# Kept-weight sums from the sorted list, shorter tie and flag arithmetic, and gathered row maxima in a top-p attention step

## The chip, the cores and the metric

The kernel runs on one core of a Trainium2 chip. A core has five engines with one instruction queue each: TensorE (PE, with its weight loads shown apart as PEld), VectorE (DVE), ScalarE (ACT), GpSimd (POOL) and SyncE (SP), which here only issues transfers. The engines wait for each other with semaphores. The metric is the device time of one execution in microseconds; the number that counts is the median of several runs.

## What is computed

The reference is a stack of four graph layers on x (4096 x 256) with a 4096 x 4096 adjacency matrix; each is followed by a residual addition and a layer norm. The change lies in the second layer, which makes two attention steps:

```python
q = X @ W1.T @ W2.T;  k = X @ W3.T
probs = softmax(q @ k.T)                        # 4096 x 4096
sp = probs sorted in falling order per row
keep_sorted = cumsum(sp) - sp < 0.9             # top-p
A = probs * mask;  A = A / max(A.sum(-1), 1e-12)
Xf = R @ Xf;  Xa = A @ Xa;  Z += Xf @ U1[n].T + Xa @ U2[n].T
```

So each row keeps its largest weights until they hold 0.9 of the mass, of several equal weights at the border only the first ones, and is divided by the sum of what it kept. The other three layers are products with the adjacency matrix, a dense product and a layer norm.

## The kernel before

**Tiles.** The 4096 rows are worked in 32 tiles of 128 rows; a row of weights `e` has 4096 columns and 24 of padding. A step n (0 or 1) is one call of `run_step` (L944). Its loop over i works on three tiles at once: logits of tile i+2 on PE (L415, copied out of PSUM by ACT, L416), selection in tile i+1, products of tile i (`pieces`, L725: transposes on PE L746, copy by ACT L749, products L769), and between them products with the adjacency rows (`neighbours`, L688, ACT cast L685) for the other term.

**Selection in a tile of step 1.** `peak_groups` (L461) takes the 8 largest of each of 18 groups of a row (MAX8, L434), and from these the row's maximum m (L466), which L467 negates for the exponential. `exp_rows` (L446) has ACT make exp(e - m) with its sum z (L457). `tops` (L518) sorts the 72 largest candidates with nine rounds of MAX8 (L529) and MATCH_REPLACE8 (L533). `pick` (L535) runs a prefix sum over them (L551), finds the border weight t (L554 to L557), the number `left` of weights equal to t that must go (L559, L560), and a flag `bad` (L563, L564, L566) that is set where the list of 72 or the eight places for ties do not suffice. `flag` (L584) counts the flagged rows with two small matmuls (L594, L595), gives each a slot (L597, L601, L602) and POOL scatters their row numbers to a list in DRAM (L608). `settle` (L643) makes up to eight copies of t out of `left` (L656 to L658), strikes as many ties out of `e` (MATCH_REPLACE8, L660), zeroes all below t in four pieces with a sum each (L665), adds the sums (L668), and `whole` (L578) turns the total into the row's factor `sc` (L580, L582). In step 0 the tiles go another way: 16 candidates are sorted, 13 neighbours gathered, and the sum `kept` comes from the list already.

**Put-off rows.** Rows flagged bad are put off into jobs of 128 rows (`put_off`, L897): one job in step 0, three in step 1, of which two run inside the loop and the last after it. `take_rows` (L883) reads 128 list entries (`to_l`, L888), limits them to a valid row number (`from_l`, L890), and gathers the rows on POOL (L812). The job computes its logits anew, takes the maximum over all 4096 columns (`peak`, L470: L472, L473), the exponential, closes in on the border with five passes of `bracket` (L475, each pass L499), sorts and picks with 64 candidates, has up to 24 tie places (three L660), and here a flag of its own (PE L590) decides a branch to a slow path. `left_over` (L924) is for more rows than the jobs hold.

**Order.** A job is a generator; `run_step` advances it by one stage at given groups of `pieces` (about L1011 to L1033). After the loop `finish` runs the last job beside 32 tiles of `zu` products (L871) for the next layer, whose operands come by SP. Within this written order a scheduler of the framework arranges the instructions of each engine when the program is built, from its own estimates of durations; the resulting order is fixed on each engine.

Of the kernel before, what the change touches and what calls it, by code (L numbers as in the profile page):

```python
# [11 lines left out]
F32 = mybir.dt.float32  # L12
# [7 lines left out]
ALU = mybir.AluOpType  # L20
AX = mybir.AxisListType
# [3 lines left out]
P = 128  # L25
# [22 lines left out]
PAD = 8 * MATCHES_LATER  # L48
# [9 lines left out]
def gnn_stack(ctx, tc, x, adjt, adjn, w0, b0, w1, w2t, w3t, u1t, u2t, ln_g, ln_b, w2, b2, w3, b3, out):  # L58
# [3 lines left out]
    nc = tc.nc  # L62
    N = x.shape[0]
    NT = N // P
# [4 lines left out]
    J0 = min(4, NT)  # L69
    BITS_LO = int(np.array(0.09 / N, np.float32).view(np.int32))  # L70

    const = ctx.enter_context(tc.tile_pool(name="const", bufs=1))
    xpool = ctx.enter_context(tc.tile_pool(name="xpool", bufs=1))
    hpool = ctx.enter_context(tc.tile_pool(name="hpool", bufs=1))
    work = ctx.enter_context(tc.tile_pool(name="work", bufs=2))
    dram = ctx.enter_context(tc.tile_pool(name="dram", bufs=1, space=DRAM))
# [46 lines left out]
    adj8_d = [dram.tile([P, NT, P], F8, name=f"adj8_{it}_d") for it in range(NT)]  # L123
    h_d = dram.tile([N + P, D], F32, name="h_d")
    k_d = dram.tile([N + P, P], F32, name="k_d")


    blank = const.tile([P, NT], I32, name="blank")
# [3 lines left out]
    def rows(t, it):  # L132
        return t[it * P : (it + 1) * P, :]
# [89 lines left out]
    with tc.tile_pool(name="l0", bufs=1) as l0, tc.tile_pool(name="l0w", bufs=2) as l0w:  # L223
# [12 lines left out]
        for c in range(NT // J0):  # L236
            t = l0.tile([P, J0, D], F32, tag="in", name="x_in", bufs=SLOTS_IN)
# [11 lines left out]
            nc.scalar.dma_start(w3t_sb[:, :, h * DA : (h + 1) * DA], w3t.rearrange("(c p) o -> p c o", p=P))  # L249
        for t in list_d:  # L250
            nc.sync.dma_start(t[:N, :].rearrange("(p k) o -> p (k o)", k=NT), blank)
        x1 = xpool.tile([P, NT, D], F32, tag="X", name="x1")
        y0h = hpool.tile([P, NT, 2 * D], F32R, tag="H", name="y0h")
        deg1 = l0.tile([P, NT], F32, name="deg1")
# [103 lines left out]
    with tc.tile_pool(name="l1", bufs=1, reuse_waits="tile") as l1:  # L358

        cur = {"late": False, "n": 0, "nef_done": False}  # L360
# [10 lines left out]
        upto = l1.tile([P, PAD], F32, name="upto")  # L371
# [45 lines left out]

        def logits_in(l):

            nc.vector.memset(l[:, N:], -1.0)  # L420
            return l

        def small(tag, w=1, dt=F32, bufs=2):
            if cur["late"]:
                return cur["lw"].tile([P, w], dt, tag=tag, name=f"{tag}_l", bufs=2 if w == 1 else 1)
            return work.tile([P, w], dt, tag=tag, name=tag, bufs=bufs)
# [15 lines left out]
        def sparse(st):  # L442

            return cur["n"] == 0 and st["tile"] is not None
# [16 lines left out]
        def peak_groups(st, ngr=ngr):  # L461

            st["cand"] = cand = small("cand", 8 * ngr, bufs=1)
            groups(st["e"], cand, ngr, -(-N // ngr))
            st["m"] = m = small("m")
            nc.vector.tensor_reduce(m, cand, axis=AX.X, op=ALU.max)  # L466
            nc.vector.tensor_scalar(m, m, -1.0, None, op0=ALU.mult)  # L467
            st["base"] = None

        def peak(st):  # L470
            st["m"] = m = small("m")
            nc.vector.tensor_reduce(m, st["e"][:, :N], axis=AX.X, op=ALU.max)  # L472
            nc.vector.tensor_scalar(m, m, -1.0, None, op0=ALU.mult)  # L473

        def bracket(st):  # L475

# [58 lines left out]
        def pick(st, rounds):  # L535

            top, thr, base = st["top"], st["thr"], st["base"]  # L540
            W = 8 * rounds
            cs = small("cs", W + 1, bufs=1)
            if base is None:
                nc.vector.memset(cs[:, 0:1], 0.0)
                te = small("te", W + 1)
                nc.scalar.activation(te, top, AF.Exp, bias=st["m"], scale=1.0)
            else:
                nc.vector.tensor_copy(cs[:, 0:1], base)
                te = top
            nc.vector.memset(cs[:, W:], 3e38)  # L550
            nc.vector.tensor_tensor_scan(cs[:, 1:W], te[:, : W - 1], te[:, : W - 1], cs[:, 0:1], op0=ALU.add, op1=ALU.max)  # L551
            under, part = small("under", W, bufs=1), small("part", W, bufs=1)
            count = small("count")
            nc.vector.tensor_scalar(under, cs[:, :W], thr, 0.0, op0=ALU.is_lt, op1=ALU.add, accum_out=count)  # L554
            nc.vector.scalar_tensor_tensor(part, cs[:, 1:], thr, under, op0=ALU.is_ge, op1=ALU.mult)
            st["t"] = t = small("t_thr")
            nc.vector.scalar_tensor_tensor(part, part, 1.0, te[:, :W], op0=ALU.mult, op1=ALU.mult, accum_out=t)  # L557
            st["left"] = left = small("left")
            nc.vector.tensor_scalar(part, te[:, :W], t, 0.0, op0=ALU.is_ge, op1=ALU.add, accum_out=left)  # L559
            nc.vector.tensor_sub(left, left, count)  # L560
            st["bad"] = bad = small("bad")
            last = KEPT if sparse(st) else W - 1
            nc.vector.tensor_tensor(bad, te[:, last : last + 1], te[:, W:], op=ALU.max)  # L563
            nc.vector.tensor_tensor(bad, bad, t, op=ALU.is_ge)  # L564
            most = 0.0 if sparse(st) else 8.0 * (MATCHES if base is None else MATCHES_LATER)
            nc.vector.scalar_tensor_tensor(bad, left, most, bad, op0=ALU.is_gt, op1=ALU.max)  # L566
            if sparse(st):

                same = small("same")
                for r in range(8, W, 8):  # L570
                    nc.vector.tensor_tensor(same, top[:, r - 1 : r], top[:, r : r + 1], op=ALU.is_equal)
                    nc.vector.tensor_tensor(bad, bad, same, op=ALU.max)
                st["w"] = w = small("w", W)
                kept = small("kept")
                nc.vector.scalar_tensor_tensor(w, te[:, :W], t, te[:, :W], op0=ALU.is_ge, op1=ALU.mult, accum_out=kept)
                whole(st, kept)

        def whole(st, kept):  # L578

            nc.vector.tensor_scalar(kept, kept, 1e-12, None, op0=ALU.max)  # L580
            st["sc"] = sc = small("sc")
            nc.vector.reciprocal(sc, kept)  # L582
# [60 lines left out]
        def settle(st, loop=False):  # L643

            e, t, left = st["e"], st["t"], st["left"]
            if loop:
                bit_by_bit(st)
            elif st.get("later") is None:
                v = nc.vector.value_load(st["nb"][0:1, 0:1])
                with tc.If(v > 0):  # L650
                    bit_by_bit(st)

            M = 8 * (MATCHES if st["base"] is None else MATCHES_LATER)
            if not loop:
                go, no, match = (small(k, PAD, bufs=1)[:, :M] for k in ("go", "no", "match"))
                nc.vector.tensor_scalar(go, upto[:, :M], left, None, op0=ALU.is_lt)  # L656
                nc.vector.tensor_scalar(no, go, -1.0, None, op0=ALU.add)
                nc.vector.scalar_tensor_tensor(match, go, t, no, op0=ALU.mult, op1=ALU.add)  # L658
                for k in range(0, M, 8):
                    nc.vector.match_replace(st["e"], match[:, k : k + 8], st["e"], 0.0)  # L660
                    yield
            kq = small("kq", NQ)
            for c in range(NQ):
                q = slice(c * QW, (c + 1) * QW)
                nc.vector.scalar_tensor_tensor(e[:, q], e[:, q], t, e[:, q], op0=ALU.is_ge, op1=ALU.mult,  # L665
                                               accum_out=kq[:, c : c + 1])
            kept = small("kept")
            nc.vector.tensor_reduce(kept, kq, axis=AX.X, op=ALU.add)  # L668
            whole(st, kept)
# [213 lines left out]
        def take_rows(n, slots, e):  # L883


            st = {"tile": None, "e": logits_in(e)}
            st["to"] = to = small("to", 1, I32)
            nc.sync.dma_start(to, list_d[n][slots, :])  # L888
            st["from"] = fr = small("from", 1, I32)
            nc.vector.tensor_scalar(fr, to, float(N - 1), None, op0=ALU.min)  # L890
            return st, gathered(xa_d if n else x1_d, st, "xf_new")

        def all_logits(st, q):
# [3 lines left out]
        def put_off(n, k, e, later):  # L897


            base = work.tile([P, 1], F32, tag="base", name="base", bufs=2)  # L900
            nc.vector.tensor_scalar(base, later["base"], float((k + 1) * P), None, op0=ALU.max)
            later["base"] = base
            st, xg = take_rows(n, slice(k * P, (k + 1) * P), e)
            yield
            q = query(xg)
            if n:
                yield
            all_logits(st, q)
            yield st
            if n == 0:  # L910
                peak_groups(st)
                exp_rows(st)
            else:
                peak(st)
                exp_rows(st)
                yield
                yield from bracket(st)
            tops(st, 8)
            pick(st, 8)
            flag(st)  # L920
            yield
            yield from settle(st)
# [309 lines left out]
```

## Time and profile before

| | |
|---|---|
| median of three runs | 3057.41 us (3055.0 to 3058.85) |
| the profiled execution, its own time | 3159.93 us |
| its span, first to last instruction | 3158.2 us |
| mean granted TensorE clock | 0.971 |
| busy: PE, DVE, ACT, POOL | 2895.0, 2247.3, 1723.6, 678.1 us |
| step 0 of the attention, about | 375 to 1260 us |
| hand-over to step 1 | 1260 to 1375 us |
| loop of step 1 | 1375 to 2450 us |
| its tail, last job and zu products | 2450 to 2605 us |
| layers 2 and 3 | 2605 to 3158 us |

The profile is of one execution, which was longer than the median by a factor of 1.0335. Times in it are from the span's start. "idle <-X" says how long an engine stood still before an instruction and what ended it; a duration is not the price of an instruction where the next one starts before it ends, so prices here are taken from start to start where two neighbours are shown.

### The profile page before, as it was taken

What the parts mean: (1) busy time and instruction counts of PE and PEld (TensorE: products, weight loads), DVE (VectorE), ACT (ScalarE), POOL (GpSimd) and SP (SyncE); (2) the same over time, 40 slices, a digit from 0 to 9 for tenths busy, and PEclk for the clock granted to TensorE, in tenths of its full rate; (3) what the DMA queues carried; (4) which work ended last, traced back from release to release, by engine and by line L of the source; (5) the groups of instructions that cost most, each with busy time, mean ns of one, the idle gap of its engine ahead of it and who ended that gap; (6) DMA issues with size and microseconds to landing.
All of it is one profiled execution on the core that took longest, in us unless ns stands there. A gap on an engine that the chain in (4) does not pass through costs nothing. (4 is left out here: it accounts for less than half of the span.)

```text
span 3158.2 us, 44761 instructions
## 1 busy us (share of the span) xinstructions
PE 2895.0 (92%) x14052; PEld 2271.4 (72%) x14052; DVE 2247.3 (71%) x7159; ACT 1723.6 (55%) x2883; POOL 678.1 (21%) x812
## 2 busy tenths in 40 slices
PE   7999888999999997789998999999999987999998
PEld 3788656777777775567777777878877645777886
DVE  4666667888888876267998999967999644444444
ACT  3555545566666654465554655546555425666664
POOL 1121245555555554000000000010000110000000
PEclk9999989999999998899999999999999998999999
DMA  9996455777777774240000111011110324333332
GB/s 172 158 178 126 77 100 110 122 131 132 128 130 136 132 133 132 79 110 17 26 23 26 30 35 38 29 36 32 34 38 24 104 92 158 108 108 95 107 109 77
DMA packets 242873, 286.82 MB, mean 91 GB/s; under 512 B 32928, under 2 KB 199776, under 8 KB 242624
## 3 DMA queue, kind: packets, MB, share of 16 engines
q0 software_dynamic: 41728, 91.69, 22.1%
q1 hardware_dynamic: 188656, 180.93, 18.6%
q10 hardware_dynamic: 12240, 11.23, 1.1%
q8 instruction: 114, 1.87, 0.2%
q14 instruction: 135, 1.11, 0.2%
HBM read 318.06 MB, written 66.32 MB: 122 GB/s over the span
## 5 line engine op out<-in xcount | busy, mean ns | idle before, releaser
L688 PE MATMUL acc_r<-xh,adjq 128*128 128x512 f32 x2048 | 625.9, 434 | 33.2 <-ACT adjq L685 17.5
L769 PE MATMUL acc_bank<-xa,at 128*128 128x256 f32 x2240 | 551.0, 386 | 26.2 <-ACT at L749 25.8
L685 ACT CAST adjq<-adj 128x512 fp32r<-128x512 fp8e4 x512 | 315.5, 619 | 371.0 <-PE acc_r L688 214.6
L688 PEld LDWEIGHTS acc_r<-xh,adjq 128*128 128x128 f32 x2048 | 382.8, 193 | 132.0 <-ACT adjq L685 37.7
L674 POOL DMA_INDIRECT G<-x_d,cols x416 | 403.5, 970 | 326.0 <-PE acc_bank L763 172.2
L769 PEld LDWEIGHTS acc_bank<-xa,at 128*128 128x128 f32 x2240 | 409.9, 193 | 85.9 <-ACT at L749 37.5
L416 ACT COPY e<-lg 128x512 f32<-128x512 f32 x544 | 315.1, 586 | 231.2 <-PE lg L415 159.9
L434 DVE MAX8 cand<-e 128x8 f32<-128x228 f32 (+1 forms) x1088 | 385.0, 399 | 34.4 <-ACT e L416 31.7
L415 PE MATMUL lg<-kS,q 128*128 128x512 f32 x1088 | 391.6, 442 | 6.0 <-issue 3.8
L200 POOL TENSOR_TENSOR rstd<-ve,mhalf 128x1 f32<-128x1 f32 x166 | 100.3, 604 | 1331.8 <-DVE ve L198 1246.3
L1112 ACT CAST a<-a 128x1024 fp32r<-128x1024 fp8e4 x256 | 268.3, 1049 | 165.4 <-PE acc L176 127.1
L531 DVE FIND_INDEX8 cols<-top,e 128x8 uint32<-128x4096 f32 x64 | 282.8, 4419 | 0.0
L176 PE MATMUL acc<-xh,a 128*128 128x512 f32 x1024 | 260.1, 407 | 21.2 <-DMA a<-adj_d 16.1
L176 PE MATMUL acc<-y0h,a 128*128 128x512 f32 x1024 | 249.9, 397 | 0.0
L176 PEld LDWEIGHTS acc<-xh,a 128*128 128x128 f32 x1024 | 191.7, 190 | 67.8 <-ACT xh L152 23.5
L176 PE MATMUL acc<-yh,a 128*128 128x512 f32 x1024 | 237.9, 394 | 0.0
L763 PE MATMUL acc_bank<-G,dg 128*128 128x256 f32 x832 | 228.1, 392 | 8.3 <-DVE dg L761 4.1
L176 PEld LDWEIGHTS acc<-yh,a 128*128 128x128 f32 x1024 | 192.2, 188 | 43.8
L176 PEld LDWEIGHTS acc<-y0h,a 128*128 128x128 f32 x1024 | 187.9, 188 | 39.0 <-issue 0.6
L749 ACT COPY at<-at_ps 128x512 f32<-128x512 f32 x288 | 168.7, 588 | 84.7 <-PE at_ps L746 83.0
L415 PEld LDWEIGHTS lg<-kS,q 128*128 128x128 f32 x1088 | 183.4, 193 | 29.6 <-ACT e L416 9.2
L763 PEld LDWEIGHTS acc_bank<-G,dg 128*128 128x128 f32 x832 | 156.3, 195 | 38.6 <-DVE dg L761 4.5
(287 smaller groups left out, 4414.1 us busy)
## 6 DMA issues: line engine op xcount, KB each, us to landing
adj<-adj_d SPq DMA_DIRECT2D x256, 128.0 KB
a<-adj_d SPq DMA_DIRECT2D x256, 128.0 KB
a<-in_adjt POOLq DMA_DIRECT2D x64, 256.0 KB
adj_d<-a SPq DMA_DIRECT2D x64, 256.0 KB
adjn<-in_adjn POOLq DMA_DIRECT2D x64, 256.0 KB
x_d<-x SPq DMA_DIRECT2D x64, 128.0 KB
xf_d<-xf_new SPq DMA_DIRECT2D x64, 128.0 KB
xf<-xf_d SPq DMA_DIRECT2D x64, 128.0 KB
```

What stands on the lines that cost most here:

```text
L176: nc.tensor.matmul(acc, a[:, j, :], halves(jt), start=(jt == 0), stop=(jt == NT - 1))
L415: nc.tensor.matmul(pl[:, :LC], q[k], kS[:, s], start=(k == 0), stop=(k == 1))
L416: nc.scalar.copy(l[:, s], pl[:, :LC])
L434: nc.vector.max(dst[:, 8 * g : 8 * g + 8], src[:, g * w : min((g + 1) * w, N)])
L531: nc.vector.max_index(st["at"][:, 8 * r : 8 * r + 8], t8, st["e"][:, :N])
L674: nc.gpsimd.indirect_dma_start(out=g, out_offset=None, in_=x1_d, in_offset=bass.IndirectOffsetOnAxis(ap=st["at"][:, k : k + 1], axis=0))
L685: nc.scalar.copy(a, cur["a8"][:, g % 2 * GP : (g % 2 + 1) * GP, :])
L688: nc.tensor.matmul(acc_r, a[:, j, :], xf[:, jt, :], start=(jt == 0), stop=False)
L749: nc.scalar.copy(at[:, :G, :], ps[:, :G, :])
L763: nc.tensor.matmul(acc_a, dg[:, k % 4, :], st["G"][k], start=(k == 0), stop=(k == KEPT - 1))
L769: nc.tensor.matmul(acc_a, ats[g][:, j, :], cur["xa"][:, jt, :], start=(jt == 0), stop=(jt == NT - 1))
L1112: nc.scalar.copy(a, a8)
```

## The change

The change has five parts, all in the second layer:

- `peak_groups` and `peak` let the reduction write the negated maximum itself, without the multiplication by -1. In step 1 `peak_groups` also writes the 128 maxima to a new tensor `m_d` in DRAM, on SP's queue; the tensor is cleared once at the start.
- `put_off` of step 1 gathers the maxima of its 128 rows from `m_d` on POOL, and `peak` isn't called there any more (`left_over` still calls it).
- `pick` computes `bad` in one instruction instead of two, and for the tiles of step 1 the sum of the kept weights from the sorted list, with `under` as mask, and `sc` from it. The four L665 of these tiles have no sum, and L668 is gone for them; jobs keep both.
- `settle` makes the tie places in one instruction (`upto < left` times t): places not used hold 0 instead of -1, and the padding of `e` is set to 0 instead of -1.
- `take_rows` limits the row number with a bitwise and instead of a minimum.

```diff
+        nc.sync.dma_start(m_d.rearrange("(p k) o -> p (k o)", k=NT), blank.bitcast(F32))
...
-            nc.vector.memset(l[:, N:], -1.0)
+            nc.vector.memset(l[:, N:], 0.0)
...
-            nc.vector.tensor_reduce(m, cand, axis=AX.X, op=ALU.max)
-            nc.vector.tensor_scalar(m, m, -1.0, None, op0=ALU.mult)
+            nc.vector.tensor_reduce(m, cand, axis=AX.X, op=ALU.max, negate=True)
+            if cur["n"]:
+                nc.sync.dma_start(rows(m_d, st["tile"]), m)
...
-            nc.vector.tensor_tensor(bad, te[:, last : last + 1], te[:, W:], op=ALU.max)
-            nc.vector.tensor_tensor(bad, bad, t, op=ALU.is_ge)
+            nc.vector.scalar_tensor_tensor(bad, te[:, last : last + 1], te[:, W:], t, op0=ALU.max, op1=ALU.is_ge)
...
+            elif st["tile"] is not None:
+                kept = small("kept")
+                nc.vector.scalar_tensor_tensor(part, under, 1.0, te[:, :W], op0=ALU.mult, op1=ALU.mult, accum_out=kept)
+                whole(st, kept)
...
-                go, no, match = (small(k, PAD, bufs=1)[:, :M] for k in ("go", "no", "match"))
-                nc.vector.tensor_scalar(go, upto[:, :M], left, None, op0=ALU.is_lt)
-                nc.vector.tensor_scalar(no, go, -1.0, None, op0=ALU.add)
-                nc.vector.scalar_tensor_tensor(match, go, t, no, op0=ALU.mult, op1=ALU.add)
+                match = small("match", PAD, bufs=1)[:, :M]
+                nc.vector.scalar_tensor_tensor(match, upto[:, :M], left, t.to_broadcast([P, M]), op0=ALU.is_lt, op1=ALU.mult)
...
+            if st["tile"] is not None:
+                for c in range(NQ):
+                    q = slice(c * QW, (c + 1) * QW)
+                    nc.vector.scalar_tensor_tensor(e[:, q], e[:, q], t, e[:, q], op0=ALU.is_ge, op1=ALU.mult)
+                return
...
-            nc.vector.tensor_scalar(fr, to, float(N - 1), None, op0=ALU.min)
+            nc.vector.tensor_scalar(fr, to, N - 1, None, op0=ALU.bitwise_and)
...
+            if n:
+                st["m"] = m = small("m")
+                nc.gpsimd.indirect_dma_start(
+                    out=m, out_offset=None, in_=m_d, in_offset=bass.IndirectOffsetOnAxis(ap=st["from"][:, 0:1], axis=0))
...
             else:
-                peak(st)
                 exp_rows(st)
```

The negation in `peak` (L472, L473) is folded in the same way. In the new file the reduction of `peak_groups` stands at L470; the lines below it are shifted by a few. The prediction uses the old numbers, and L470 for that reduction where it speaks of the write to `m_d`.

More of the change, by code (lines that the diff above doesn't have):

```diff
@@ L70, in gnn_stack @@
     BITS_LO = int(np.array(0.09 / N, np.float32).view(np.int32))
+    assert N & (N - 1) == 0
     const = ctx.enter_context(tc.tile_pool(name="const", bufs=1))
@@ L125, in gnn_stack @@
     k_d = dram.tile([N + P, P], F32, name="k_d")
+    m_d = dram.tile([N, 1], F32, name="m_d")
     blank = const.tile([P, NT], I32, name="blank")
@@ L471, in peak @@
             st["m"] = m = small("m")
-            nc.vector.tensor_reduce(m, st["e"][:, :N], axis=AX.X, op=ALU.max)
-            nc.vector.tensor_scalar(m, m, -1.0, None, op0=ALU.mult)
+            nc.vector.tensor_reduce(m, st["e"][:, :N], axis=AX.X, op=ALU.max, negate=True)
         def bracket(st):
@@ L572, in pick @@
                     nc.vector.tensor_tensor(bad, bad, same, op=ALU.max)
+            elif st["tile"] is not None:
+                kept = small("kept")
+                nc.vector.scalar_tensor_tensor(part, under, 1.0, te[:, :W], op0=ALU.mult, op1=ALU.mult, accum_out=kept)
+                whole(st, kept)
+            if sparse(st):
                 st["w"] = w = small("w", W)
```

## The prediction

> **What bounds the kernel now.** I first read the page's busy times, because they say which engine can matter at all.
>
> ```profile
> PE 2895.0 (92%) x14052; PEld 2271.4 (72%) x14052; DVE 2247.3 (71%) x7159; ACT 1723.6 (55%) x2883; POOL 678.1 (21%) x812
> ```
>
> TensorE (PE) is busy 92% of the span, VectorE (DVE) 71%; by this average no DVE edit would count. The average hides the stages, so next come the stretches. Columns: length, then busy time of PE, PEld, DVE, ACT, POOL with counts, granted clock, DMA share.
>
> ```profile
> 375.00:1260.00 885.00, 790.88 (x4223) 606.99 (x4221) 698.86 (x2100) 516.77 (x1001) 476.63 (x512) 0.95 0.70 127
> 1448.00:1682.00 234.00, 216.25 (x1139) 181.56 (x1139) 213.53 (x746) 121.13 (x202) 18.05 (x24) 1.00 0.08 24
> 1988.00:2064.00 76.00, 74.36 (x389) 62.53 (x388) 73.53 (x264) 44.28 (x74) 5.91 (x7) 1.00 0.09 28
> 2440.00:2605.00 165.00, 147.00 (x601) 96.09 (x599) 94.00 (x208) 56.55 (x115) 22.04 (x20) 0.98 0.28 95
> 2605.00:3158.00 553.00, 517.98 (x2240) 413.43 (x2240) 245.42 (x656) 330.97 (x425) 36.18 (x65) 0.97 0.35 109
> ```
>
> The rows are: attention step 0; eight tiles of step 1 ahead of any put-off job; three tiles between two jobs; the tail of step 1; layers 2 and 3. In step 1 PE and DVE are both nearly full. In the second row both have about 20 us of holes in 234, so the two wait for each other in a ring; in the third row DVE has 2.5 us free in 76 and PE 1.6, so what DVE saves, PE can use only up to its own holes. In the tail DVE has much room, but one chain of it is what PE ends up waiting for. The last row is untouched.
>
> Then the groups by line, for step 1 with its hand-over: which DVE work is there to take.
>
> ```profile
> L665 DVE SCALAR_TENSOR_TENSOR e<-e,t_thr 128x1024 f32<-128x1024 f32 x128 | 159.0, 1276 | 0.0
> ...
> L472 DVE TENSOR_REDUCE m_l<-e 128x1 f32<-128x4096 f32 x3 | 13.3, 4420 | 23.9 <-ACT e L416 23.9
> ```
>
> The timeline of DVE in a tile without a job shows the chain that the change shortens; the durations overlap, so prices are read from start to start.
>
> ```profile
> 1505.71 0.23 DVE L656 TENSOR_SCALAR go<-upto,left 128x8 f32<-128x8 f32 x1
> 1505.97 0.17 DVE L657 TENSOR_SCALAR no<-go 128x8 f32<-128x8 f32 x1
> 1506.18 0.23 DVE L658 SCALAR_TENSOR_TENSOR match<-go,t_thr,no 128x8 f32<-128x8 f32 x1
> 1506.51 0.09 DVE L660 MATCH_VALUE_LOAD e<-match,e 128x8 f32 x1
> ```
>
> Last the tail's timeline, of DVE and of PE, around the last put-off job.
>
> ```profile
> 2458.45 0.15 DVE L890 TENSOR_SCALAR from_l<-to_l 128x1 int32<-128x1 int32 x1 [7.23 <-DMA to_l<-list_d]
> ...
> 2475.57 4.42 DVE L472 TENSOR_REDUCE m_l<-e 128x1 f32<-128x4096 f32 x1 [10.71 <-ACT e L416]
> 2480.02 0.15 DVE L473 TENSOR_SCALAR m_l<-m_l 128x1 f32<-128x1 f32 x1
> 2484.10 0.15 DVE L459 TENSOR_SCALAR thr_l<-z_l 128x1 f32<-128x1 f32 x1 [3.93 <-ACT e L457]
> ...
> 2535.12 0.16 DVE L566 SCALAR_TENSOR_TENSOR bad_l<-left_l,bad_l 128x1 f32<-128x1 f32 x1
> ```
>
> ```profile
> 2535.33 0.19 PE L590 MATMUL mm_bank<-ones_col,bad_l 128*1 128x1 f32 x2 [1.41 <-DVE bad_l L566]
> ...
> 2566.89 1.04 PE L746 MATMUL at_ps<-ident,e 128*128 128x128 f32 x8
> ```
>
> Logits are done at 2475.6, then 4.4 us row maximum, 3.9 us exponential (ACT), 51 us bisection and sorting, then the flag matmul L590. PE fills this time with other work in a written order, waits 1.41 us at L590, and does 31.4 us more before the job's products at 2566.9.
>
> **What the Trainium skill says.** "Vector Engine (DVE) Microarchitecture Reference", section 5.2, gives 1.0417 ns per column plus about 75 ns per instruction; 1024 columns would be 1.14 us. The trace has 1.20 from start to start, and 1.20 for L513 too, which has no accumulator; so dropping the accumulator of L665 gains nothing, although the page shows a separate read of 83 ns. "DMA: Bandwidth & Descriptors", "Anatomy of one DMA", puts about 2 us on every transfer, mostly the receipt; here a scatter, its receipt and the read back (L608 at 2447.30 to L890 at 2458.45) take 11.2 us. "TensorE: Matmul & The Clock Gate", "What's actually happening", halves the clock after an idle window of about 3.4 us; the trace agrees: after a PE gap of 4.00 us at 2088.5 eight L769 matmuls took 3.78 us instead of 1.89.
>
> **The change part by part**, from start-to-start times and from the order of instructions of the two programs, which is fixed when they are built.
>
> *Tiles without a job* (about 8). The chain L564 (1505.33) to L660's load (1506.51) loses L657 (0.21), L656 and L658 become one (about 0.3), L563/L564 become one; the new sum (72 wide, like L557: 0.23, with a read) stands in gaps of the chain and takes back about 0.15. Ahead of it L467 goes (0.12). Ring shorter by 0.5: 8 x 0.55 = -4.4.
>
> *Dense tiles* (about 16). Saved pitches: L467 0.12, L563/564 0.06, L656/657/658 0.23, L668 0.08; added 0.18 for the sum. -0.3 x 16 = -4.8, all usable only if PE's holes (about 1 us a tile) give way. Those of L594, which waits for "bad", give least: the new sum stands just ahead of L566.
>
> *Step 0.* L467 and L564 of 32 tiles, 0.13 a tile, PE waits about 1 us a tile on flags: -2, at most -4.
>
> *Row maxima* (3 times 4.42). In the two jobs inside the loop DVE's next instructions in the new order are thr_l and the first probe, ahead of the tile's last maxima; they wait for the exponential, 3.9 us. So 4.4 us of work turn into 3.9 us of waiting: -0.5 each, -1. Also ACT now runs this exponential straight after the logits, ahead of the copies of the transposed pieces (at, L749) that PE needs; PE has about 2 us of neighbour products to bridge 3.9: +1.5 each, +3, perhaps with half clock after it.
>
> *Maxima to DRAM and back.* 32 writes of 512 bytes, 0.32 us each on SP's queue; SP is idle most of the loop. Behind each waiting write stand loads of adj and xf, which were issued many us ahead: 0, and 0.3-2 each if that cover is gone. Two writes also wait for the gather; it ends (1 us, plus 2 us receipt) before SP's next load was issued in either place: 0. L470's buffer is reused two tiles (50 us) later, so its wait for the old write is covered: 0. Three gathers on POOL, about 1.0 us like L812: hidden under the logits (15 us and more) where they stand behind xf_new; in the second job ahead of xf_new, whose next user comes 24 us later: 0.
>
> *Cover of the list read.* In the second job six maxima instead of nine stand between the slots and from_l, where DVE stalls 5.2 us already: 3 x 0.35, +1. In the tail L847, L848 and all four L665 stand ahead of the slots, L602: some 2 us later by pitches, half regained because L824 no longer stands ahead of L660: +1, on a PE hole that exists (1.97 us).
>
> *Flag in the tail.* bad_l comes 4.4 + 0.15 + 0.1 = 4.7 us earlier (2530.4). But the new PE order puts L590 two groups of zu products (eight L871 and their transposes, 4.65 us each) earlier. PE waits there for bad_l, then has 31.4 + 9.3 = 40.7 us to do: 2571.3 instead of 2566.9 (L590 itself 0.2): +4.8 with rounding. The settling of e (2537.65 to 2556) had 11 us to spare and keeps them. What is late next is the last products, the write of zu_d, and layer 2 behind it.
>
> Rest (bitwise_and, memset 0.0, bad in one): nothing; same pitch.
>
> Sum: -4.4 -4.8 -2 -1 +3 +1 +1 +4.8 = -2.4 us on an execution of 3159.93 us (span 3158.2), which stands 1.0335 times above the median of the runs, 3057.41. So -2.3: 3055.
>
> **Rivals.**
> (1) *DVE is the bound all through step 1* and everything taken from it comes off: 0.5 x 8 + 0.6 x 20 + 13.3 us of maxima is 29, less 5 for the sum and the tail's order: 24 us, 3034. For it: DVE idles under 1 us in dense tiles. Against: PE idles no more there, and 3.9 of each 4.4 is replaced by a wait.
> (2) *Slower: the last job's flag.* If the loop's small savings vanish in PE's order (PE has 0.04 to 1.2 us of holes in a dense tile) the tail decides: +4.8, its cover +2, clock at half after the wait (2 us more), and the exponential ahead of the copies +3 to +5: 3057 + 12 = 3069. It decides as soon as the loop gives under 6 us.
> (3) *Nothing:* PE order bound, savings and losses under 3 us: 3057. This lies beside my forecast.
>
> **How the numbers follow.** 0.2%, about what a measurement of this kernel can tell from no change, is 6.1 us. Forecast (loop gains and tail losses nearly cancel; its own range 3047 to 3063): 0.45, a third of it below 3051.3. Rival 1 (3028 to 3045): 0.25. Rival 2 (3062 to 3080): 0.27. Rest 0.03. Faster 0.25 + 0.15 = 0.40; same 0.31; slower 0.29. Bounds of unknown terms: gains up to -24, losses up to +14 with 0.1 left out on each side: 3035 to 3072.
>
> **What would show it.** Right: tiles without a job take 28.7 instead of 29.3 us; DVE idles 3.9 us for the exponential at each job, where L472 stood; L590 near 2531 relative to logits at 2475.6, with a PE wait of 3 to 6 us before it, and L746 4 to 5 us later. Wrong: PE waits for adj or xf loads behind the writes on SP; dense tiles shorter by more than 1 us; or bad_l not 4.7 us earlier.

## The result and the profile after

The changed kernel takes 3066.3 us (median of ten runs, 3062.86 to 3070.95), the kernel before, timed beside it, 3057.94 us (ten runs, 3055.0 to 3061.32): ratio 1.0024, 95% interval 1.0016 to 1.0033. So the change makes the kernel 8.4 us slower. A repetition (run 18 below) gave 3068.89 against 3058.3 us, ratio 1.0038 [1.0025, 1.0052]. The forecast was 3055 us, with faster as the likeliest sign; the nearest case was rival 2 (slower, 3069).

The page of the changed kernel first. Its execution took 3062.86 us with a span of 3061.2.

```profile
PE 2852.7 (93%) x14052; PEld 2259.7 (74%) x14052; DVE 2216.9 (72%) x6852; ACT 1725.1 (56%) x2883; POOL 705.5 (23%) x815
```

PE's count is that of before; DVE has 307 instructions fewer (6852 against 7159). These totals can't be set against the page of before: in that profile step 0 of the attention takes 810 us, and here it takes 723. The runs below show that chips differ by that much in this one stage, whatever the kernel (see the last section). The profile of before therefore seems to come from another kind of chip than the times. For stages I use a trace of the kernel before and one of the changed kernel, taken one after the other on one chip like that of the result (runs 17 and 18 below). Each row is a stretch: length, busy time of PE, PEld, DVE, ACT and POOL with counts, clock, DMA share. In order: step 0 from its first to its 32nd flag, hand-over to the first flag of step 1, loop of step 1 up to its last flag, tail from there up to layer 2. The kernel before:

```profile
405.90:1123.60 717.70, 703.06 (x3997) 556.62 (x3995) 655.99 (x1995) 484.50 (x937) 455.87 (x489) 0.99 0.81 142
1123.60:1292.40 168.80, 128.80 (x536) 97.10 (x536) 76.92 (x217) 79.42 (x133) 16.75 (x16) 0.85 0.38 113
1292.40:2345.20 1052.80, 992.24 (x5039) 821.75 (x5038) 927.74 (x3184) 571.12 (x954) 76.28 (x98) 0.99 0.12 31
2345.20:2527.20 182.00, 147.46 (x601) 96.53 (x599) 96.04 (x211) 61.89 (x120) 23.02 (x21) 0.93 0.31 103
```

The changed kernel:

```profile
402.00:1122.70 720.70, 705.46 (x3997) 559.12 (x3995) 653.24 (x1936) 485.26 (x937) 459.48 (x492) 0.99 0.81 142
1122.70:1294.20 171.50, 129.65 (x536) 97.91 (x536) 75.33 (x207) 79.93 (x134) 15.36 (x15) 0.85 0.37 111
1294.20:2346.40 1052.20, 990.93 (x5041) 823.66 (x5039) 917.57 (x2968) 566.55 (x954) 99.08 (x100) 0.99 0.14 31
2346.40:2529.80 183.40, 148.66 (x602) 97.27 (x600) 82.85 (x195) 62.21 (x120) 24.02 (x22) 0.93 0.30 102
```

DVE gets 10 us of work off in the loop and 13 in the tail, and neither stage gets shorter: -0.6 and +1.4. Step 0 and the hand-over get longer, +3.0 and +2.7. Layers 2 and 3 take the same (537.0 and 536.7). What lies ahead of step 0's first flag is not touched by the change but for one small write, and single traces on such chips differ there by up to 9 us. Run 17's own execution was 7.6 us above the median beside it, and its first flag is late (405.9 us, against 397 to 403 in the six changed kernels on such chips). So the spans of these two traces are not to be compared, only their stages.

Now the three places that the prediction looked at. First DVE in a tile without a job, changed kernel: start, duration, line.

```profile
1407.80 0.35 DVE L555 TENSOR_TENSOR_SCAN cs<-te,cs 128x71 f32<-128x71 f32 x1
...
1409.91 0.22 DVE L664 SCALAR_TENSOR_TENSOR match<-upto,left,t_thr 128x8 f32<-128x8 f32 x1
1410.23 0.09 DVE L666 MATCH_VALUE_LOAD e<-match,e 128x8 f32 x1
```

The same two ends in the kernel before (run 17):

```profile
1408.49 0.35 DVE L551 TENSOR_TENSOR_SCAN cs<-te,cs 128x71 f32<-128x71 f32 x1
...
1411.43 0.09 DVE L660 MATCH_VALUE_LOAD e<-match,e 128x8 f32 x1
```

One instruction (L664) stands where three stood (L656 to L658). From the start of the scan to the load of the match's values it is now 2.43 us, where the kernel before takes 2.94. Second, PE in the tail, where PE's last logits end at 2372.4:

```profile
2372.62 1.04 PE L757 MATMUL at_ps<-ident,e 128*128 128x128 f32 x8
2377.57 2.78 PE L780 MATMUL acc_bank<-xa,at 128*128 128x256 f32 x8 [3.92 <-ACT at L760]
...
2428.27 0.19 PE L598 MATMUL mm_bank<-ones_col,bad_l 128*1 128x1 f32 x2 [1.68 <-DVE bad_l L569]
...
2469.14 1.04 PE L757 MATMUL at_ps<-ident,e 128*128 128x128 f32 x8
```

PE stands 3.92 us, does eight products (L780) in 2.78 us, waits 1.68 us for the flag, and needs 40.7 us from the end of the flag to the job's products. In the kernel before, PE waited 1.41 us for the flag and needed 31.4. From the end of the logits to the products it is 96.8 us now, where it was 92.0. Third, the cause of the 3.92 us, on ACT:

```profile
2373.24 3.71 ACT L461 ACTIVATE e<-e,m_l 128x4096 f32<-128x4096 f32 x1
2376.93 1.08 ACT L760 COPY at<-at_ps 128x512 f32<-128x512 f32 x2
```

The exponential of the last job no longer waits for a row maximum, so it stands ahead of the two copies that PE needs. The same happens once more, near the end of the loop, to an ordinary tile's exponential; there PE loses more, with its clock down for the eight products after it (3.78 us where they take 1.89 elsewhere):

```profile
2319.84 1.04 PE L757 MATMUL at_ps<-ident,e 128*128 128x128 f32 x8
2326.21 3.78 PE L780 MATMUL acc_bank<-xa,at 128*128 128x256 f32 x8 [5.34 <-ACT at L760]
```

### The profile page after: what moved, and what is told of

It is laid out like the page before. It is cut to its first block, busy times and chain, and to the rows that moved or that the text cites. A ratio compares the mean times of both kernels' runs of the same rounds, so it can differ in the third digit from the quotient of the medians.

```text
span 3061.2 us, 44561 instructions
## 1 busy us (share of the span) xinstructions
PE 2852.7 (93%) x14052; PEld 2259.7 (74%) x14052; DVE 2216.9 (72%) x6852; ACT 1725.1 (56%) x2883; POOL 705.5 (23%) x815
## 5 line engine op out<-in xcount | busy, mean ns | idle before, releaser
L780 PE MATMUL acc_bank<-xa,at 128*128 128x256 f32 x2240 | 549.7, 385 | 30.3 <-ACT at L760 29.7
L780 PEld LDWEIGHTS acc_bank<-xa,at 128*128 128x128 f32 x2240 | 409.1, 193 | 89.2 <-ACT at L760 41.4
L438 DVE MAX8 cand<-e 128x8 f32<-128x228 f32 (+1 forms) x1088 | 374.2, 397 | 42.5 <-ACT e L420 40.8
L203 POOL TENSOR_TENSOR rstd<-ve,mhalf 128x1 f32<-128x1 f32 x166 | 100.7, 606 | 1270.2 <-DVE ve L201 1233.8
```

The costliest lines, as they stand in the source:

```text
L438: nc.vector.max(dst[:, 8 * g : 8 * g + 8], src[:, g * w : min((g + 1) * w, N)])
L780: nc.tensor.matmul(acc_a, ats[g][:, j, :], cur["xa"][:, jt, :], start=(jt == 0), stop=(jt == NT - 1))
```

## The experiments

Theory at the start: in step 1 the small edits gain, and the gathered row maxima take the gain back through the order of instructions. Rivals: the change is worth nothing anywhere (PE's order alone decides); the flag's place alone makes the loss. To compare step 1 between chips, three stretches are read from each trace: **A** from the first flag of step 1 to the end of the last job's logits on PE, **B** from there to that job's products, **C** from there to the first product of layer 2.

| kernel (run) | A | B | C | step 0 + hand-over |
|---|---|---|---|---|
| before (shown profile, 1, 5, 13, 17) | 1087.5, 1087.9, 1091.0, 1082.0, 1088.2 | 92.0 | 53.8 to 55.0 | 979.0, 980.3, 973.8, 967.5, **886.5** |
| whole change (result, 6, 18) | 1081.7, 1084.7, 1083.3 | 96.8 | 54.9 to 55.8 | **893.4**, 965.2, **892.2** |
| maxima alone (2) | 1079.7 | 96.9 | 55.5 | 973.9 |
| without maxima (3, 7) | 1073.7, 1074.4 | 91.7 | 54.7, 56.0 | 972.3, 968.8 |
| ties and flag alone (8) | 1077.7 | 92.0 | 56.4 | 974.2 |
| query behind products (4) | 1079.5 | 96.8 | 55.1 | 978.2 |
| exponentials behind copies (9) | 1081.9 | 94.8 | 53.7 | **898.3** |
| flag back (10) | 1085.4 | 95.4 | 53.5 | **896.1** |
| without maxima, query behind (11) | 1069.1 | 91.7 | 54.5 | **899.8** |
| all three orders mended (12) | 1073.6 | 91.2 | 55.2 | **900.5** |
| as 12, maxima written by POOL (15) | 1073.2 | 91.2 | 54.5 | 963.6 |
| whole, maxima written by POOL (16) | 1082.4 | 96.9 | 55.7 | 966.3 |
| whole in step 1, step 0 as before (14) | 1077.3 | 96.8 | 55.0 | 970.4 |

(us; bold: chips like that of the result, where step 0 is some 80 us shorter. A differs by up to 9 us between traces of one kernel, B by 0.1. A starts at a flag and the loop in the stage rows above ends at one, so their differences are not the same: the last flag stands 31 us ahead of the logits' end in the changed kernel and 35 before.)

**Runs 1 to 4: parts of the change.** The kernel before again, for a trace; the row maxima alone; everything but the row maxima; the whole change with the query moved. The maxima alone are this part of the diff (with the bitwise and):

```diff
+            nc.vector.tensor_reduce(m, cand, axis=AX.X, op=ALU.max, negate=True)
+            if cur["n"]:
+                nc.sync.dma_start(rows(m_d, st["tile"]), m)
...
+            if n:
+                st["m"] = m = small("m")
+                nc.gpsimd.indirect_dma_start(
+                    out=m, out_offset=None, in_=m_d, in_offset=bass.IndirectOffsetOnAxis(ap=st["from"][:, 0:1], axis=0))
...
-                peak(st)
                 exp_rows(st)
```

The kernel without maxima has all the rest. For the fourth, an edge in the order puts a tile's query behind all four products of its group in the tiles without a job, where the changed kernel had put it behind three, and the next logits behind the query:

```diff
+                            with tc.issue_after(cur["prod"].ins):
+                                cur["qs"].append(query(None, turned[0]))
...
+                    with tc.issue_after(cur.pop("asked").ins):
+                        logits_chunk(nxt["e"], nxt["q"], g)
```

> The kernel before, once more, for a second trace, since its first profiled execution was 100 us longer than the median and spent them in step 0 of the attention. Both theories: 3055 to 3062 us, step 1 as in the first trace (1245.9 us from its first struck ties to the first matmul of layer 2, give or take 2).

> Only the maxima part of the change: negated reductions, maxima to DRAM, gathered by the put-off jobs, no row maximum there. Theory A (the loss comes with the maxima: the late exponential stands ahead of the copies of the transposed pieces, and the last flag is early): slower than before by 5 to 12 us. Theory B (the loss comes with the shorter tie and flag arithmetic, which makes the scheduler place the query two matmuls earlier): within 3 us of before.

> The change without the maxima part: sums from the sorted list, tie places and flag in one instruction each, negated reductions; the jobs compute their row maxima. Theory A: 0 to 6 us faster than before. Theory B: slower than before by 4 to 9 us.

> The whole change, with the query of nine tiles ahead of the jobs put back behind its group of products (order only, no work changed). Theory: in these tiles the DVE chain is 0.5 us shorter, and the two matmuls that the new order has behind the query's wait give 0.43 of it back; with them in front again a tile takes 28.8 us instead of 29.2, and the run is 3 to 4 us faster than the changed kernel: 3062 to 3063. Rival (the ring is bound elsewhere): no change, 3066.

Before 3159.6 us on this chip. Maxima alone: 0.9975 [0.996, 0.9991]. Without maxima: 0.9947 [0.9931, 0.9963]. Whole change with the query moved: 0.9963 [0.995, 0.9976]. The maxima alone came out faster, which neither theory expected, and the kernel without them is the fastest of the three by more than theory A allowed (17.6 us instead of 0 to 6). In step 1 A and B show it: both are 5 to 6 us shorter than in the two kernels with maxima.

The fourth run settles where the job-free tiles' gain went. PE at the query in the kernel before (L395, run 17):

```profile
1413.49 1.89 PE L769 MATMUL acc_bank<-xa,at 128*128 128x256 f32 x8
1416.33 0.71 PE L395 MATMUL mm_bank<-xt,wq_sb 128*128 128x128 f32 x4 [0.95 <-DVE h L824]
```

in the changed kernel (L399):

```profile
1383.29 1.46 PE L780 MATMUL acc_bank<-xa,at 128*128 128x256 f32 x6
1385.92 0.71 PE L399 MATMUL mm_bank<-xt,wq_sb 128*128 128x128 f32 x4 [1.17 <-DVE h L835]
1386.47 0.60 PE L780 MATMUL acc_bank<-xa,at 128*128 128x256 f32 x2
```

and with the edge (run 4):

```profile
1478.70 1.89 PE L783 MATMUL acc_bank<-xa,at 128*128 128x256 f32 x8
1481.34 0.71 PE L399 MATMUL mm_bank<-xt,wq_sb 128*128 128x128 f32 x4 [0.75 <-DVE h L838]
```

Eight matmuls are the four products of a group. In the change's order two of these matmuls stand behind the query, which waits 1.17 us for h (DVE's sum ahead of the layer norm); ahead of it they fill part of that wait (0.75 us left). A tile without a job takes 29.27 us before, 29.2 with the change, 28.80 with the edge. So the chain on DVE did get shorter by what was predicted, and the reshuffled query gave 0.4 of the 0.5 us back. The reorder comes with the edits of ties and flag: it is in runs 3 and 8, and the maxima alone don't have it.

**Runs 5 to 8: again, and the ties alone.** Run 8 has only the edits of `match`, `bad` and the padding.

> The kernel before, for a trace beside the next three. Chips differ: in the earlier traces step 0 (from the first to the 32nd count of flagged rows, L594) took 810 and 808 us with the kernel before on chips where it runs 3160 us, and 723 us with the changed kernel where it runs 3066. On a chip with 3057 us for the kernel before: step 0 near 715 us if the loss of 8 us lies in step 0, near 723 if it lies elsewhere.

> The whole change, beside its parts on the same chip. Theory A (the maxima part costs, in step 1's tail, on every chip): slower than before by 5 to 10 us on any chip, 10 us or more slower than the change without the maxima. Theory C (the loss lies in step 0, where the gathers' latency differs from chip to chip): on a chip with 3160 us for the kernel before it is faster than before by 5 to 15 us, on one with 3057 slower by 8.

> The change without the maxima part, again. On a chip with 3160 us for the kernel before: 12 to 20 us faster than before, as the first time. On one with 3057: theory A 2 to 10 us faster; theory C (step 0 loses through the merged flag and negation, which this kernel has too): 0 to 8 us slower.

> Only the tie places and the flag in one instruction each, with the padding at 0. This is the part that has the two products behind the query, and the shorter flag in step 0. Theory A: within 5 us of the change without the maxima. Theory C: it carries what step 0 loses or gains; its step 0 is as that of the whole change within 3 us.

Before 3152.24 us. Whole change 0.9997 [0.9986, 1.0009]; without maxima 0.9943 [0.9926, 0.9959]; ties alone 0.9955 [0.9939, 0.9972]. On this chip the whole change is level, neither slower nor faster, which neither theory of run 6 expected. Without the maxima A is 13 us shorter than before, and with them 9 us of it are gone and B is 5 us longer. Maxima alone gain, ties alone gain, and together they don't. Whether the order that they bring about on PE and ACT decides is what runs 9 to 12 test.

**Runs 9 to 12: the orders mended.** Run 9 holds a put-off job's exponential behind the second copy of its group; this brings the ordinary tile's exponential back behind its copies too. Run 10 puts the last job's flag behind the two groups of zu products again. Run 11 is the kernel without maxima with run 4's edge. Run 12 is the whole change with all three edges, and a fourth for the ordinary tile's exponential.

```diff
-                exp_rows(st)
+                with tc.issue_after(cur["turns"][1].ins):
+                    exp_rows(st)
...
-            flag(st)
+            if n and k == LATER[n] - 1:
+                with tc.issue_after(cur["zus"][17].ins):
+                    flag(st)
```

> The whole change, with one order edge added: the exponential of a put-off job may not be issued before the second copy of transposed pieces of its group (this also puts the last ordinary tile's exponential back behind its two copies). Theory A (the row maxima part loses its gain through the order on ACT): the two PE gaps of 5.3 to 6.0 us near the end of the loop and 3.9 us in the tail, and the half-clocked products behind them, go; the loop of step 1 falls from 1053.5 to about 1047, the sum of step 1 from its first flag to layer 2 from 1236.3 to about 1227, ratio to before about 0.997. Theory B (the maxima's own transfers, waits and the reshuffled job iterations cost it): the gaps go, but the sum stays at 1232 or more, ratio 0.999 to 1.000.

> The whole change, with the last job's flag matmul put back behind the two groups of zu products that the new order has put after it; nothing else moves. The prediction's step (the earlier place of the flag costs 4.8 us by itself): from the end of the job's logits to its products 96.2 falls to 91.4. Theory A (the exponential ahead of the copies costs the tail its time, and the flag's place only the 1.68 us that PE waits for it): 94.5. Loop of step 1 unchanged, 1050 to 1054; ratio against the kernel before 0.998 to 1.000.

> The change without the row maxima (sum of kept weights, ties, overflow flag, negated maxima), and the query of the job-free tiles behind its group's four products. If the two effects add: tiles without a job 29.19 falls to 28.8, the loop of step 1 from 1042.5 to about 1039, ratio to before 0.9945 falls to about 0.9935. If DVE's other work in those tiles takes it back: 0.9945.

> The whole change with all three orders mended: exponentials behind the copies, flag back, query behind the products. Theory A: with the order mended the row maxima are worth a little by themselves, sum of step 1 about 1220, ratio 0.9935 to 0.995, as the kernel without maxima. Theory B: 1228 or more, ratio 0.996 to 0.998, so that the maxima part costs more than its order.

Before 3066.61 us on this chip. Ratios: 0.9976 [0.9964, 0.9987], 1.0012 [1.0003, 1.0021], 0.9948 [0.9934, 0.9962], 0.9964 [0.9949, 0.9979]. In run 12 ACT's copies stand ahead of the exponential, as in run 9, and PE's gap is 0.29 us:

```profile
2375.31 1.07 ACT L761 COPY at<-at_ps 128x512 f32<-128x512 f32 x2
2376.27 3.72 ACT L461 ACTIVATE e<-e,m_l 128x4096 f32<-128x4096 f32 x1
```

```profile
2375.95 1.99 PE L784 MATMUL acc_bank<-xa,at 128*128 128x256 f32 x8 [0.29 <-ACT at L761]
2433.55 0.19 PE L598 MATMUL mm_bank<-ones_col,bad_l 128*1 128x1 f32 x2
```

B tells the two causes in the tail apart. Whole change 96.8; flag back 95.4 (the prediction's own step had -4.8, theory A -1.7; it is -1.4); exponential behind the copies 94.8; both 91.2. The query's edge alone leaves B at 96.8 (run 4). Each alone brings 1.4 to 2.0 us, both bring 5.6, because they cover each other: with the flag alone put back PE still loses its 3.9 us, and with the exponential alone put back PE comes to the flag earlier, waits 2.36 us there, and still has 37.6 us to do behind it. So neither the flag's place nor the exponential's is the cause by itself.

In the loop run 9 fell short of its expectation: both gaps go, but A gets only about 1 us shorter than the whole change's, and the first two tiles of step 1 take 78.7 us there instead of 76. Run 12 has a step 1 (A + B + C) of 1220.0, the whole change 1235.4 on average (1234.3 to 1236.4), run 11 1215.3. Of the whole change's excess over run 11, by these traces, the orders that no edit asked for make 15 us; 5 remain with the maxima. For the 15 there are traces alone, as the whole change was not run on this chip. The 5 lie within the spread of A, but the medians of runs 11 and 12, from one chip, say the same: 3051.8 and 3057.49. Theory A of run 12 had the sum right, and missed the ratio. Run 11 shows the two effects adding up in the loop (A 1069.1, against 1073.7 and 1074.4 in runs 3 and 7); ratios of different kinds of chips can't be compared.

**Runs 13 to 16: the first two tiles, and step 0.** With maxima the first two tile periods of step 1 (from the first tile's struck ties to the third's) take 75.7 to 79.0 us, without 74.2, before 73.2. SP's waits in the first 80 us of the loop, changed kernel (line waited at, what it waited for, sum, times, longest):

```profile
SPq L694 <- ACT adjq L696: 40.5, 20, 7.6
SPq L472 <- DVE top L533: 19.5, 2, 18.8
```

Theory Q read the 18.8 us as the first write's, with loads held up behind it. So runs 15 (run 12) and 16 (the whole change) send the writes through POOL's queue. Run 14 takes the edits of step 0 out of the whole change. Run 13 is the kernel before.

```diff
-                nc.sync.dma_start(rows(m_d, st["tile"]), m)
+                nc.gpsimd.dma_start(rows(m_d, st["tile"]), m)
```

> The kernel before, for the trace of its step 0 beside those of the changed kernels. On a chip on which the kernel before takes some 3060 us: theory S (the change's edits in step 0 cost there what they gain elsewhere) expects the step-0 loop, from the first flag to the last, at 716 to 720 us, against 723 to 728 in the changed kernels' traces; theory N (step 0 is untouched) expects 723 to 728.

> The whole change, but in step 0 the row maximum is negated and the overflow flag is made in two instructions each, as before. Theory S: on a chip on which the kernel before takes some 3060 us this is 5 to 8 us faster than the whole change (ratio to before 0.999 to 1.000, where the whole change had 1.0024), on one of some 3155 us it is slower than the whole change by as much. Theory N: the same time as the whole change within 3 us.

> Twelfth experiment's kernel, with the row maxima written to DRAM through POOL's queue instead of SP's. Theory Q (the first maxima's writes, which wait up to 18.8 us on SP, hold up the adjacency loads behind them and so PE): the first two tiles' periods fall from 79.0 to about 74.5 us, the sum of step 1 from 1220 to about 1215, ratio to before 0.994 to 0.996, level with the kernel without maxima. Rival R (the loads are late for another reason, such as the share of the DMA engines): 79 and 1220.

> The whole change, with the row maxima written through POOL's queue instead of SP's; the order of the other engines as it is in the change. Theory Q: the first two tiles' periods fall from 75.7 to 77.1 us to about 74, the loop of step 1 by 2 to 3 us to about 1048. Rival R: nothing.

Before 3147.78 us on this chip, so one with the long step 0: run 13 could not show the short one, and run 14 (0.9989 [0.998, 0.9997]) could not tell the theories apart, as the whole change was not run beside it and the chip was of the other kind. Run 15: 0.9916 [0.9896, 0.9936]; run 16: 0.9965 [0.9952, 0.9977].

Theory Q does not hold for the changed kernel. In run 15 the first two tiles fall from 79.0 to 76.3 us, but A stays (1073.6 and 1073.2); in run 16 they stay at 76.3, where the whole change had 75.7 to 77.1. SP's own timeline in the changed kernel says why:

```profile
1323.28 0.32 SPq L725 DMA_DIRECT2D xf_d<-xf_new  x1
1342.07 0.32 SPq L472 DMA_DIRECT2D m_d<-m  x1
1350.07 0.32 SPq L694 DMA_DIRECT2D adj<-adj_d  x1
```

The 18.8 us are the third tile's write, which stands at an otherwise idle queue. The load behind it starts 7.7 us after the write's end: it waits for ACT to free its buffer (the 7.6 in the first line of the waits). Behind the first two writes, which wait under 1 us, the next load starts 4.1 us after them, again when ACT frees a buffer. So here the writes hold up no load, and what makes the first two tiles longer with maxima is not settled. The two ratios are better than A, B and C explain: the program's end became 6 us shorter, which is told below.

**Runs 17 and 18: step 0 on a chip like that of the result.**

> The kernel before once more, for its step 0 on the same chip as the whole change of the next run. Theory N (the edits in step 0 are worth nothing there): the loops of step 0 of the two agree within the spread of such traces, some 5 us, on whatever chip. Theory S: on a chip with about 3060 us the kernel before is 5 to 8 us faster in step 0.

> The whole change once more. From the sum of step 1 in traces (1234.3 to 1236.3 against 1228.1 to 1238.0 before) ratio 0.998 to 1.001; theory S: 1.0024 again where the kernel before takes about 3060 us.

Before 3058.3 us, whole change 3068.89 us: 1.0038 [1.0025, 1.0052]. Here the chip has the short step 0. All waits of PE in it that the view lists, kernel before:

```profile
PE nef_ps L698 <- DMA adjn<-in_adjn: 3.6, 2, 3.1
PE acc_bank L763 <- DMA G<-x_d,cols: 3.2, 3, 2.3
PE acc_bank L763 <- DVE dg L761: 2.6, 1, 2.6
PE mm_bank L822 <- ACT xt L188: 2.4, 1, 2.4
PE tr L186 <- DMA xf<-xf_d: 2.1, 1, 2.1
```

And from step 0 in the shown profile of before, lines for the flag of a tile (L594):

```profile
PE mm_bank L594 <- DVE bad L572: 6.5, 4, 3.6
PE mm_bank L594 <- DVE kept L580: 5.5, 5, 1.3
...
PE mm_bank L594 <- DVE dg L761: 3.9, 4, 1.0
PE mm_bank L594 <- issue: 3.8, 4, 1.0
...
PE mm_bank L594 <- DVE bad L566: 2.6, 2, 1.3
```

PE waits 14 us in all in the first, and not once for a flag; 69 us in the second, 22 of it ahead of L594, of which 15 were ended by a value of the flag (`bad`, `kept`). So on such a chip there is nothing in step 0 for a shorter chain to gain.

What the edits cost there is less clear. The loop of step 0 takes 717.7 us before and 720.7 with the change, which lies within the 5 us that theory N of run 17 allowed, while the ratio speaks for theory S. With the hand-over it is 886.5 and 892.2, and 893.4 to 900.5 in the five other traces of changed kernels from such chips. The six changed traces have 720.7 to 727.6 us in step 0 alone. PE's busy time there, for the same matmuls, is 705.5 to 708.2 us in them and 703.1 before; it stands 15 to 21 us and 14.6 before. In the hand-over PE's wait for the put-off job's settled e grew from 8.2 to 9.9 us and that for dg, a product of weights on DVE, from none to 11.4, in place of 10.2 at L688.

There is one trace of before from these chips, so the medians must help. Take from each kernel's difference of medians what A + B + C show against the mean of before (1233.8). What remains is +8 and +9 us for the whole change (result, run 18) and -2 to +5 in runs 9 to 12, all on chips with the short step 0. On the others it is -3 to -8 in the eight kernels with edits in step 0 (in runs 15 and 16 without the 6 us of the program's end), and +2 or +3 in run 14, which has step 0 as before. Layers 2 and 3 agree within 4 us in all of them. So the edits in step 0 gain where PE waits for flags, and the whole change loses in step 0 and the hand-over where it doesn't. That a new order of the instructions is the cause there is likely, but no run shows it: run 14 was not made on such a chip.

## Why the prediction was wrong

By its own steps; before stands for the mean of five traces, after for that of three (A 1087.3 and 1083.2).

| step | predicted | measured |
|---|---|---|
| tiles without a job, eight | -4.4 | -0.6 (234.0 to 233.4); -3.6 with the query moved |
| rest up to the end of the last logits: dense tiles, jobs, covers, writes | -0.8 | -3.5, of it +1 ahead of the eight tiles |
| flag in the tail | +4.8 | +4.8 (92.0 to 96.8) |
| products to layer 2 | 0 | +0.9 |
| step 0 with hand-over | -2 | +5.7 (runs 17, 18) |
| sum | -2.4 | +7.3; medians +8.4, +10.6 |

- **The step that failed is step 0.** "PE waits about 1 us a tile on flags: -2": on the chips of the timed runs PE doesn't wait for flags there at all (14 us of other waits in run 17), so a shorter chain could gain nothing. The stage with its hand-over lost 5.7 us by the traces, 8 to 9 by the medians. That loss was not foreseen, and which instruction makes it stays open. The waits were read off a profile in which they exist, and even there they are 0.7 us a tile. The warning was on the page: the profiled execution stood 1.0335 times above the median, and I scaled by that factor as if it lay on everything alike. Most of it lay in step 0 (810 against 718 us), while step 1, A + B + C, is 1233.3 in that trace and 1234.9 in run 17's.
- **Tiles without a job: mechanism right, place wrong.** The chain is 0.4 to 0.5 us shorter as worked out. That PE would pass it on was wrong: the ties edit moved the query ahead of the last of its group's four products. The prediction followed the new order for flags, exponentials and gathers, and left this one out.
- **Dense tiles and jobs: size.** Measured -4.6 us without the stretch ahead of the eight tiles, predicted -0.8. PE's holes there were put at 1 us a tile; the row shown for three tiles has 0.5. Which edit brings the gain was not separated. That A as a whole comes near the prediction (-5.2 predicted, -4.1 measured) is luck: two errors cancel.
- **Row maxima.** Right that DVE waits for the exponential instead, and that ACT runs it ahead of the copies. I priced this for the two jobs in the loop at 1.5 us each, where PE now waits 1.1 and 0.9 behind it. I left it out in the tail, where PE loses 3.9 us, and for the ordinary tile's exponential, where it loses 5.3 and half the clock.
- **Writes of the maxima: predicted 0, and 0 as far as is shown.** In the changed kernel each transfer behind such a write is released only after the write has gone out; at the loop's start the loads wait for ACT to free their buffers. Moving the writes to POOL (run 16) leaves A within its spread.
- **Flag in the tail: sum right, in part by luck.** bad_l, the two groups and the 40.7 us are as worked out. But the flag put back alone returns only 1.4 us; the other 3.4 hang on the exponential's place as well.

Rival 2 came nearest in time. Its point ("as soon as the loop gives under 6 us") was met: up to the logits' end step 1 gives 4.1 us and the tail takes 5.7, about half of what the rival had. Step 1 as a whole is thus 1.6 us slower, within the spread of A. Step 0 and the hand-over do the rest, which no rival had, so that the rival's time came near is luck. Rival 1 is out: DVE lost 23 us of work in loop and tail, and step 1 got no shorter.

## What to carry over

Before costing a stage by the waits of a profile, see whether that execution is as long as the median, and if not, find the stage that holds the difference; a saving that rests on waits in that stage is not to be had where the waits are absent. Where a scheduler writes the order, each edit's own gain (here 0.5 us a tile) is of the size of one matmul pair that it moves across a wait; list every instruction that changes sides of a wait, not only those the edit names, and hold the good places by an explicit order edge. A long wait of a queue is not yet a cost: see what the next transfer behind it waited for, and when.

A faster kernel than both came out: without the row maxima and with the query behind its products (run 11), 0.9948 [0.9934, 0.9962], on a chip where before takes 3066.61. With the maxima, all orders mended and their writes on POOL (run 15) it is 0.9916 [0.9896, 0.9936], measured only on a chip with the long step 0.

## What the runs showed of the hardware

- **Chips differ in one stage.** Step 0 of the unchanged kernel takes 798 to 811 us in four traces from other chips and 717.7 in run 17, with the same bytes moved (run 13: 101.65 MB at 127 GB/s; run 17: 101.90 at 142) and the same mean duration of POOL's gather issue (973 and 975 ns). Of the 80.6 us between runs 13 and 17, 30 are PE's busy time (733.3 us at a granted clock of 0.97, 703.1 at 0.99) and 50 are time that PE stands. Step 1 and layers 2 and 3 agree within 1%. Each chip was used at one time only, so chip and time are not separated, and what makes the difference stays open.
- **The end of the program.** In all kernels but two, the one before included, the span ends 8.6 to 8.9 us after the last write of the result was issued (3048.18 to 3057.1 in run 12). In runs 15 and 16, which write the maxima through POOL, it is 2.8 us (3116.90 to 3119.7, 3136.69 to 3139.5). Why the use of POOL's queue shortens it is open. It makes up 6 of the 25 us by which run 15 beats the kernel before.
- **The clock after a gap.** "TensorE: Matmul & The Clock Gate", section "What's actually happening", in the Trainium skill has the clock halved after an idle window of about 3.4 us. Here eight products take 3.78 us after 5.34 us of standing and 2.78 after 3.92, against 1.89, and the granted clock over them is 0.50 and 0.69. So the traces agree, and in the second case half clock held for a part of the eight only.
